# A two-block transformer on one core: the planner's clock gets a time for each change of the array's shape, products run in columns also behind scores, normed inputs use a form with two tensors

## The chip, the core and the metric

The kernel runs on one core of a Trainium2 chip. The core has TensorE (PE: matmuls, with its weight loads shown as PEld), VectorE (DVE), ScalarE (ACT), GpSimd (POOL) and SyncE (SP), which here issues the DMAs. The metric is the device time in microseconds of one execution; the median of three runs is given. Lower is better.

## What is computed

Two blocks, one after the other, over x of 32 samples x 128 tokens x 256 channels, in float32, with 16 heads of 16 channels. Each has self-attention, cross-attention to a context of 128 tokens, and a feed-forward layer with 1024 hidden channels:

```python
# block 0 (modulated by silu(cond) @ ada_w + ada_b)
xm1 = ln(x) * (1 + scale_sa) + shift_sa
x = x + gate_sa * (attn(qkv of xm1) @ sa_proj_w + sa_proj_b)
x = x + (attn(q of ln(x), k and v of context, mask) @ ca_proj_w + ca_proj_b)
x = x + gate_ff * (gelu(xm3 @ fc1_w + fc1_b) @ fc2_w + fc2_b)   # xm3: ln(x), modulated
# block 1 (gamma, beta from cond; rotated q and k)
x = x + attn(rope(q), rope(k), v of adaln1(x)) @ sa_out_w.T
x = x + attn(rope(q of adaln2(x)), rope(k), v of context) @ ca_out_w.T
x = x + (gelu(adaln3(x) @ ffn_w1.T + ffn_b1) @ ffn_w2.T + ffn_b2)
# ln(x) = (x - mean) / sqrt(var + eps); attn is a softmax over 128 keys
```

## The kernel before

The 32 samples are 16 groups of two (256 token columns each). A group goes through a block as a stream; eight streams are under way at once, on eight sets of buffers. Each stream is a Python generator that yields whenever it needs an engine. At building, a planner (`Tasks.run`, lines 150 to 176) keeps all waiting steps, asks a model clock (`Clock`, lines 42 to 102) when each could start, and emits the step that could start first; so the order of every engine's instructions is fixed before the kernel runs, and the chip only keeps its dependencies. For every 40 us of planned time a number of the table `ORDER` (line 35) seeds small changes of rank (`changed`) and, by `seed % 4`, a patience: how much later than the earliest a step may start and still be chosen by rank.

What the clock charges on TensorE depends on the shape in which the array is used:
- **full**: a 128x128 tile. `multiply` (line 258) writes the products of weights and activations this way at L264; transposes of normed inputs (L586) and of score maxima (L774) are also full.
- **rows**: 32x128 tiles. The scores (L749): four heads stand on 32 partitions each, 16 matmuls for one batch and pass.
- **columns**: 128x32 tiles. exp times values (L795), and products that follow them: at L262 `multiply` splits a product into four matmuls of 32 output partitions.

A step whose shape is "any" takes columns if the array is in columns, otherwise full:

```python
if way == "any":
    way = "columns" if self.way == "columns" else "full"
took = took * self.PACE + (self.TURN[self.way] if way != self.way else 0.0)
```

`rows_T`, `values` and `project` use it; a long row of products behind exp times values therefore stays in columns until something else comes.

Attention of one sample and one stage runs twice through one shared scores buffer of four PSUM banks: scores (L749), maxima by VectorE (L761), their transpose (L774), subtraction from the queries (L778), scores again in the other direction (L749), exp by ScalarE (L787), exp times values (L795), copy out by ScalarE (L801). The sums of the softmax go through DMAs (a strided copy, L818's reciprocal, a store and a broadcast load) before L829 multiplies them in. Four PSUM buffers (`mms`) are shared by all products and transposes.

Before each stage `normed_T` (from line 554) norms x: statistics on VectorE (L561, L562), the power -1/2 on GpSimd (L566, L568), then for each of two samples x minus mean times the reciprocal deviation on VectorE (L574), and `transposed` transposes the four 128x128 parts on TensorE (L586); L604, L606 or L596 write them to SBUF.

The trace shows a float32 product as two matmul records (eight in columns), and 32 records for a group of 16 score matmuls; a transpose has one.

Of the kernel before, what the change touches and what calls it, by code (L numbers as in the profile page):

```python
# [13 lines left out]
ALU = mybir.AluOpType  # L14
# [3 lines left out]
P = 128  # L18
B, S, D, H, HD, DF = 32, 128, 256, 16, 16, 1024
# [13 lines left out]

EVERY = 40.0
ORDER = (
    71372, 36752, 0, 0, 71454, 91697, 0, 94157, 73524, 26634, 81926, 67541, 0, 14443, 0, 59342, 0, 88828, 0,
    12337, 30536, 2421, 29624, 8901, 84470, 22357, 96881, 43920, 51881, 25816, 98785, 9044, 8412, 0, 96954, 9117,
    0
)


class Clock:

    HOP, DRAIN, TABLE, PACE = 0.06, 0.22, 1.28, 1.03
    TURN = {"full": 0.1, "rows": 0.15, "columns": 0.15}

    def __init__(self):
        self.free = dict.fromkeys(("pe", "dve", "act", "pool", "sp", "none"), 0.0)  # L50
        many = {"sc": 1, "mm": 4, "pt": 2, "set": NA, "qa": 2, "ou": 3, "st": 2, "ht": 1,
                "y": 3, "cx": 3, "x": NS + 1}
        self.slots = {kind: [0.0] * n for kind, n in many.items()}
        self.table, self.way = None, "full"
        self.now = 0.0
        self.moved = 0.0
        self.landed = 2.0

    def use(self, engine, took, way="full"):

        if engine in ("exp", "gelu"):
            if engine != self.table:
                took += self.TABLE
                self.table = engine
            engine = "act"
        if engine == "pe":
            if way == "any":
                way = "columns" if self.way == "columns" else "full"
            took = took * self.PACE + (self.TURN[self.way] if way != self.way else 0.0)
            self.way = way  # L70
        self.free[engine] = max(self.now, self.free[engine]) + took
        return self.free[engine] + (self.DRAIN if engine == "pe" else self.HOP)

    def dma(self, took):

        start = max(self.now, self.free["sp"])
        self.free["sp"] = start + 0.64
        self.moved = max(self.moved, start + 0.9) + max(0.1, took - 1.4)
        return self.moved + 0.5
# [40 lines left out]
def when(t):  # L120
    return t() if callable(t) else t
# [6 lines left out]
class Tasks:  # L128
# [21 lines left out]
    def run(self):  # L150
        clock = self.clock
        while self.waiting:

            first, chosen = {}, {}
            at = int(min(t for e, t in clock.free.items() if e in ("pe", "dve", "act")) / EVERY)
            seed = ORDER[at] if at < len(ORDER) else 0
            patience = (0.02, 0.02, 0.3, 0.8)[seed % 4]
            for task in self.waiting:
                ready, engine, kinds, rank = task[1]
                start, late = max(when(ready), clock.slot(kinds)), 0.0  # L160
                if engine in ("exp", "gelu"):
                    late = 0.0 if engine == clock.table else clock.TABLE
                    engine = "act"
                start = max(start, clock.free[engine])
                first.setdefault(engine, []).append((start, late, rank, task))
            for engine, l in first.items():
                horizon = min(start + late for start, late, _, _ in l)
                l = [(late, self.changed(task, rank, seed), task[2].turn(), start, i) for i, (start, late, rank, task) in enumerate(l)
                     if start + late <= horizon + patience]
                late, _, _, start, i = min(l)  # L170
                chosen[engine] = (start, first[engine][i][3])
            start, task = min(chosen.values(), key=lambda c: c[0])
            assert start < NEVER
            clock.now = start
            self.waiting.remove(task)
            self.step(task)
# [54 lines left out]
def two_blocks(ctx: ExitStack, tc: tile.TileContext, a: dict, out: bass.AP):  # L231
    nc = tc.nc
# [8 lines left out]
    clock = Clock()  # L241
# [15 lines left out]

    def multiply(to, lhs, rhs, start=True, stop=True):

        if clock.way == "columns":  # L260
            for j in range(0, P, 32):
                nc.tensor.matmul(to[j:j + 32], lhsT=lhs[:, j:j + 32], rhs=rhs, start=start, stop=stop)  # L262
        else:
            nc.tensor.matmul(to, lhsT=lhs, rhs=rhs, start=start, stop=stop)  # L264
# [51 lines left out]
    rows = const.tile([P, C + 2], F32, name="rows")  # L316
# [237 lines left out]
    def normed_T(wm, x, ready, eps, mod, g, name):  # L554


        mv = p_s.tile([P, GB, 2], F32, tag="mv", name=f"mv_{name}")
        yield ready, "dve", "", 1
        for b in range(GB):
            st = p_s.tile([P, 6], F32, tag="st", name=f"st_{name}_{b}")  # L560
            nc.vector.bn_stats(st, x[:, b, :])  # L561
            nc.vector.bn_aggr(mv[:, b, :], st)  # L562
        t = clock.use("dve", 1.17)
        yield t, "pool", "", 1
        ve = p_s.tile([P, GB], F32, tag="ve", name=f"ve_{name}")
        nc.gpsimd.tensor_scalar(ve, mv[:, :, 1], eps, None, ALU.add)  # L566
        rstd = p_s.tile([P, GB], F32, tag="rstd", name=f"rstd_{name}")
        nc.gpsimd.tensor_tensor(rstd, ve, neg_half, ALU.pow)  # L568
        t = clock.use("pool", 1.0)
        yield t, "dve", "y", 0  # L570
        y = clock.take("y")
        xn = ys[y]
        for b in range(GB):
            nc.vector.tensor_scalar(xn[:, b, :], x[:, b, :], mv[:, b, 0:1], rstd[:, b:b + 1],  # L574
                                    ALU.subtract, ALU.mult)
        t = clock.use("dve", 0.75)
        return (yield from transposed(wm, y, t, mod, g))

    def transposed(wm, y, t, mod, g):
        to, xn = wm.xt, ys[y]  # L580
        yield (lambda: when(t) if mod is None or mod in mods else NEVER), "pe", "mm", 1
        slot = clock.take("mm")
        ps = mms[slot].rearrange("p (c b s) -> p c b s", c=KC, s=S)
        for c in range(KC):
            for b in range(GB):
                nc.tensor.transpose(ps[:, c, b, :], xn[:, b, c * P:(c + 1) * P], ident)  # L586
        t = clock.use("pe", 0.45)
        clock.give("y", y, t)
        there = Event()

        def evict():

            engine = "act" if mod is None else clock.freer("act", "dve")
            yield t, engine, "", 1
            if mod is None:
                nc.scalar.copy(to.rearrange("p c (b s) -> p c b s", s=S), ps)  # L596
            else:
                scale, shift = mods[mod]
                for c in range(KC):
                    for b in range(GB):  # L600
                        at = g * GB + b
                        one, by, to_add = to[:, c, b * S:(b + 1) * S], scale[:, c, at:at + 1], shift[:, c, at:at + 1]
                        if engine == "act":
                            nc.scalar.activation(one, ps[:, c, b, :], AF.Identity, bias=to_add, scale=by)  # L604
                        else:
                            nc.vector.tensor_scalar(one, ps[:, c, b, :], by, to_add, ALU.mult, ALU.add)  # L606
            clock.give("mm", slot, there.add(clock.use(engine, 0.6 if mod is None else 1.45)))

        tasks.spawn(evict(), wm)
        return there  # L610
# [128 lines left out]
    def attention(wm, hd, masked, t, t_v, name, done):  # L739
# [3 lines left out]
        turned_top, second = [Event() for _ in range(GB)], [Event() for _ in range(GB)]  # L743
# [9 lines left out]
        def batch(b):  # L753
# [4 lines left out]
            end = group_rows(scs[slot], lambda p, c: q[p, c, cut], lambda p, c: k[p, c, cut])  # L758
# [13 lines left out]
                ou.append(clock.take("ou"))  # L772
            ps = mms[at][:, 0:S]
            nc.tensor.transpose(ps, top.rearrange("p r i -> p (r i)"), ident)  # L774
            end = turned_top[b].add(clock.use("pe", 0.12) + 0.1)
            yield end, "dve", "", 0
            qa = qas[less]
            nc.vector.tensor_tensor(qa, q[:, :, cut], ps.unsqueeze(1).to_broadcast([P, C, S]), ALU.subtract)  # L778
            end = clock.use("dve", 0.7)
# [3 lines left out]
            end = second[b].add(group_rows(scs[slot], lambda p, c: k[p, c, cut], lambda p, c: qa[p, c, :]))  # L783
# [4 lines left out]
            end = clock.use("exp", 1.98)  # L788
# [9 lines left out]
            end = last.add(clock.use("pe", 0.87, "columns") + 0.1)  # L798
# [3 lines left out]
            end = clock.use("act", 0.6)  # L802
# [30 lines left out]
        for b in range(GB):  # L833
            tasks.spawn(batch(b), wm)
# [301 lines left out]
```

## Time and profile before

| | us |
|---|---|
| median of 3 runs | 1459.13 (1456.2 to 1461.75) |
| the profiled execution | 1462.32 |
| its span, first to last instruction | 1460.5 |
| first matmul record, start of the last one | 1.3, 1455.9 |

The span is that of the instructions; the execution's time has a little around it. The page's chain of work that ended last lies 83% on TensorE. The costliest groups, by busy time in us, count and mean:

| group | busy | count | mean ns |
|---|---|---|---|
| DVE L761, maxima of scores | 300.6 | 256 | 1216 |
| ACT L787, exp | 248.3 | 256 | 1023 |
| PE L264, second feed-forward product | 193.4 | 848 | 382 |
| PE L749, scores, the two directions | 151.1 and 150.8 | 4096 each | 284 |
| PE L795, exp times values | 139.0 | 4096 | 278 |
| DVE L778, queries less maxima | 86.1 | 128 | 675 |
| POOL L729, rotated sums | 83.0 | 64 | 1299 |

A matmul's duration in this trace is modelled and overlaps with the next, so the distance from start to start is what counts on TensorE. Busy times of groups are unions: an operation that began while the one ahead was still running is not counted twice.

### The profile page before, as it was taken

Reading aid. Unit: us, or ns where it says so; the run is one execution under the profiler, and the core shown is the slowest. Engines: PE = TensorE matmul, PEld = TensorE weight load, DVE = VectorE, ACT = ScalarE, POOL = GpSimd, SP = SyncE. Lnnn points to the kernel's source line nnn. Section 1 sums busy time; section 2 is a strip of 40 time slices with the busy share of each in tenths; the row PEclk is TensorE's granted clock in tenths of the full one; section 3 lists DMA queues with packets and bytes.
Section 4 is the critical chain, followed back from the end, with each engine's and each line's share of the span. In section 5 each row is a group of like instructions: output and inputs, shape, how many; then the busy total and the mean of one; then the engine's idle time right before and its main releaser. Section 6 shows DMA issues by size and latency. Waiting matters only on the chain.

```text
span 1460.5 us, 45118 instructions
## 1 busy us (share of the span) xinstructions
PE 1425.4 (98%) x19764; PEld 1136.3 (78%) x19764; DVE 889.2 (61%) x1538; ACT 707.5 (48%) x1130; POOL 357.2 (24%) x498
## 2 busy tenths in 40 slices
PE   9999999999999999999999999999999999999998
PEld 7877778877777777667877777878788788777777
DVE  6656575665655665646565667667756557664641
ACT  6544464465465545445444544434454444535452
POOL 3122213332223314331223222122121212111111
PEclk9999999999999999999999999999999999999999
DMA  7253222233122242223313313032122212321110
GB/s 229 79 157 86 68 75 70 82 102 103 50 75 65 82 125 86 85 64 96 111 50 117 121 57 108 30 98 93 62 68 74 81 45 67 100 74 43 49 61 22
DMA packets 107380, 120.85 MB, mean 83 GB/s; under 512 B 11632, under 2 KB 82992, under 8 KB 107184
## 3 DMA queue, kind: packets, MB, share of 16 engines
q1 hardware_dynamic: 107184, 117.98, 26.1%
q8 instruction: 155, 2.54, 0.7%
q14 instruction: 41, 0.34, 0.1%
HBM read 54.92 MB, written 12.68 MB: 46 GB/s over the span
## 4 chain that ended last, share of the span: by engine, by line
PE 83%; DVE 6%; DMA 5%; ACT 2%; POOL 2%; issue 1%; SPq 1%; DVEq 0%; ACTq 0%; POOLq 0%
PE products L264 42%; PE scores L749 16%; PE products L262 11%; PE products L795 7%; PE products L586 3%; DVE top L761 2%; PE products L774 1%; DMA y<-gate_dram_sa 1%; ACT exp L787 1%; DVE y L574 1%; DMA ou<-inv_e 1%; DVE st L724 1%; DVE xt L829 1%; DMA ou<-inv_a 1%; PE products L475 1%
## 5 line engine op out<-in xcount | busy, mean ns | idle before, releaser
L761 DVE TENSOR_REDUCE top<-scores 128x8 f32<-128x1024 f32 x256 | 300.6, 1216 | 63.1 <-PE scores L749 60.2
L787 ACT ACTIVATE exp<-scores 128x1024 f32<-128x1024 f32 x256 | 248.3, 1023 | 168.3 <-PE scores L749 157.6
L264 PE MATMUL products<-w_ffn_w,ht 128*128 128x256 f32 x848 | 193.4, 382 | 0.0
L893 ACT ACTIVATE ht<-products,cols 128x256 f32<-128x256 f32 x256 | 117.2, 474 | 129.8 <-PE products L264 113.9
L264 PE MATMUL products<-xt,w_ffn_w 128*128 128x256 f32 x760 | 176.7, 383 | 0.4 <-DVE x L869 0.4
L264 PEld LDWEIGHTS products<-w_ffn_w,ht 128*128 128x128 f32 x848 | 158.5, 190 | 23.1
L749 PEld LDWEIGHTS scores<-qa,keys 32*128 32x128 f32 x4096 | 126.7, 187 | 48.1 <-issue 23.3
L749 PE MATMUL scores<-qa,keys 32*128 32x128 f32 x4096 | 151.1, 284 | 7.3 <-ACT exp L787 3.5
L264 PEld LDWEIGHTS products<-xt,w_ffn_w 128*128 128x128 f32 x760 | 140.8, 190 | 22.2 <-DVE x L869 0.8
L801 ACT COPY ou<-products 128x512 f32<-128x512 f32 x128 | 75.5, 591 | 166.7 <-PE products L795 157.9
L749 PEld LDWEIGHTS scores<-keys,queries 32*128 32x128 f32 x4096 | 126.4, 187 | 37.3 <-issue 19.5
L749 PE MATMUL scores<-keys,queries 32*128 32x128 f32 x4096 | 150.8, 284 | 3.3 <-ACT exp L787 3.2
L729 POOL TENSOR_TENSOR st<-st 128x512 f32<-128x512 f32 x64 | 83.0, 1299 | 234.1 <-DVE st L724 223.0
L795 PE MATMUL products<-exp,values 128*32 128x128 f32 x4096 | 139.0, 278 | 0.0
L778 DVE TENSOR_TENSOR qa<-queries,products 128x512 f32<-128x512 f32 x128 | 86.1, 675 | 66.3 <-PE products L774 65.7
L795 PEld LDWEIGHTS products<-exp,values 128*32 128x32 f32 x4096 | 106.7, 110 | 22.8 <-issue 11.1
L869 DVE TENSOR_TENSOR x<-products,x 128x512 f32<-128x512 f32 x64 | 43.9, 688 | 103.9 <-PE products L264 75.9
L829 DVE TENSOR_TENSOR xt<-xt,ou 128x512 f32<-128x512 f32 x64 | 49.3, 770 | 87.3 <-DMA ou<-inv_d 29.8
L724 DVE TENSOR_TENSOR st<-products,rope 128x512 f32<-128x512 f32 x128 | 81.4, 680 | 23.8 <-PE products L264 8.2
L264 PE MATMUL products<-xt,w_qkv_w 128*128 128x256 f32 x336 | 83.2, 394 | 0.8 <-DVE xt L606 0.8
L644 ACT COPY values<-products 128x512 f32<-128x512 f32 x64 | 40.4, 631 | 89.5 <-PE products L264 70.8
L877 POOL TENSOR_TENSOR x<-y,x 128x512 f32<-128x512 f32 x32 | 40.8, 1276 | 164.1 <-DVE y L873 164.0
(129 smaller groups left out, 1970.8 us busy)
## 6 DMA issues: line engine op xcount, KB each, us to landing
xt<-ou SPq DMA_DIRECT2D x64, 256.0 KB, 2.4
keys<-st SPq DMA_DIRECT2D x96, 128.0 KB, 2.1
queries<-st SPq DMA_DIRECT2D x96, 128.0 KB, 2.2
cxt<-in_ctx SPq DMA_DIRECT2D x32, 256.0 KB, 3.7
x<-in_x SPq DMA_DIRECT2D x16, 256.0 KB, 4.1
keys<-st SPq DMA_DIRECT2D x16, 256.0 KB, 2.7
y<-gate_dram_sa SPq DMA_DIRECT2D x16, 256.0 KB, 3.8
ou<-inv_a SPq DMA_DIRECT2D x32, 128.0 KB, 2.6
```

What stands on the lines that cost most here:

```text
L262: nc.tensor.matmul(to[j:j + 32], lhsT=lhs[:, j:j + 32], rhs=rhs, start=start, stop=stop)
L264: nc.tensor.matmul(to, lhsT=lhs, rhs=rhs, start=start, stop=stop)
L724: nc.vector.tensor_tensor(st[:, :, :, one], ps[:, :, one].unsqueeze(2).to_broadcast([P, 2, 2, S]), rope, ALU.mult)
L729: nc.gpsimd.tensor_tensor(st[:, 0], st[:, 0], st[:, 1], ALU.add)
L749: nc.tensor.matmul(sc[:, r, c * S:(c + 1) * S], lhsT=lhs(slice(32 * r, 32 * r + 32), c), rhs=rhs(slice(32 * r, 32 * r + 32), c), start=Tru ...
L761: nc.vector.tensor_reduce(top[:, r:r + 2, TOP:TOP + 2 * C:2], scs[slot][:, r:r + 2, :].rearrange("p r (c s) -> p r c s", s=S), AX.X, ALU.max)
L778: nc.vector.tensor_tensor(qa, q[:, :, cut], ps.unsqueeze(1).to_broadcast([P, C, S]), ALU.subtract)
L787: nc.scalar.activation(exps[pt][r // 2], scs[slot][:, r:r + 2, :], AF.Exp, scale=SCALE)
L795: nc.tensor.matmul(mms[at][32 * r:32 * r + 32, c * S:(c + 1) * S], lhsT=v[:, b, i:i + HD, :].rearrange("p d t -> p (d t)"), rhs=exps[pt][r ...
L801: nc.scalar.copy(ous[ou[0]][:, :, cut], mms[at].rearrange("p (c s) -> p c s", s=S))
L829: nc.vector.tensor_tensor(wm.xt, wm.xt, by, ALU.mult)
L893: nc.scalar.activation(ht[f // (FC // 2)][:, f % (FC // 2), :], ps[:, 0, :], AF.Gelu, bias=b1[:, f:f + 1])
```

## The change

Three things, in one diff. The clock's table of changes gets one time for each pair of shapes instead of one for each shape that is left, with two more shapes: "parts" (products in columns) and "turned" (transposes, which leave the array full); the general factor on TensorE's times goes from 1.03 to 1.015, and the table of seeds is another one. A product takes columns also if the array is in parts or, in stretches of 40 us whose seed asks for it (`lean`), if it stands in rows. And the normed inputs are computed by scalar_tensor_tensor: (x - mean) times the reciprocal deviation, the latter read as a tensor of 256 equal columns instead of as a scalar of each partition. Lines behind the edits move down: L264 is L275 in the changed kernel, L262 L273, L574 L586, L586 L598, L749 L761, L774 L786, L787 L799, L795 L807.

```diff
 ORDER = (
-    71372, 36752, 0, 0, 71454, 91697, 0, 94157, 73524, 26634, 81926, 67541, 0, 14443, 0, 59342, 0, 88828, 0,
...
+    38718, 32014, 0, 87893, 99950, 56838, 0, 53341, 21925, 7768, 6954, 0, 63578, 91846, 41557, 5424, 0, 45477, 0,
...
-    HOP, DRAIN, TABLE, PACE = 0.06, 0.22, 1.28, 1.03
-    TURN = {"full": 0.1, "rows": 0.15, "columns": 0.15}
+    HOP, DRAIN, TABLE, PACE = 0.06, 0.22, 1.28, 1.015
+    TURN = {
+        ("full", "rows"): 0.1, ("full", "columns"): 0.1, ("full", "parts"): 0.1,
+        ("rows", "full"): 0.26, ("rows", "turned"): 0.18, ("rows", "columns"): 0.15, ("rows", "parts"): 0.15,
+        ("columns", "full"): 0.26, ("columns", "turned"): 0.18, ("columns", "rows"): 0.15,
+        ("parts", "full"): 0.32, ("parts", "turned"): 0.24, ("parts", "rows"): 0.21,
+    }
...
-        self.table, self.way = None, "full"
+        self.table, self.way, self.lean = None, "full", False
...
             if way == "any":
-                way = "columns" if self.way == "columns" else "full"
-            took = took * self.PACE + (self.TURN[self.way] if way != self.way else 0.0)
-            self.way = way
+                way = "parts" if self.in_parts() else "full"
+            took = took * self.PACE + self.TURN.get((self.way, way), 0.0)
+            self.way = "full" if way == "turned" else way
...
+    def in_parts(self):
+
+        return self.way in ("columns", "parts") or self.way == "rows" and self.lean
...
             patience = (0.02, 0.02, 0.3, 0.8)[seed % 4]
+            clock.lean = seed // 4 % 4 == 3
...
-        if clock.way == "columns":
+        if clock.in_parts():
             for j in range(0, P, 32):
                 nc.tensor.matmul(to[j:j + 32], lhsT=lhs[:, j:j + 32], rhs=rhs, start=start, stop=stop)
...
-            nc.vector.tensor_scalar(xn[:, b, :], x[:, b, :], mv[:, b, 0:1], rstd[:, b:b + 1],
-                                    ALU.subtract, ALU.mult)
+
+            nc.vector.scalar_tensor_tensor(xn[:, b, :], x[:, b, :], mv[:, b, 0:1],
+                                           rstd[:, b:b + 1].to_broadcast([P, D]), ALU.subtract, ALU.mult)
...
-        t = clock.use("pe", 0.45)
+        t = clock.use("pe", 0.45, "turned")
...
-            end = turned_top[b].add(clock.use("pe", 0.12) + 0.1)
+            end = turned_top[b].add(clock.use("pe", 0.12, "turned") + 0.1)
```

More of the change, by code (lines that the diff above doesn't have):

```diff
@@ L35 @@
 ORDER = (
-    71372, 36752, 0, 0, 71454, 91697, 0, 94157, 73524, 26634, 81926, 67541, 0, 14443, 0, 59342, 0, 88828, 0,
-    12337, 30536, 2421, 29624, 8901, 84470, 22357, 96881, 43920, 51881, 25816, 98785, 9044, 8412, 0, 96954, 9117,
-    0
+    38718, 32014, 0, 87893, 99950, 56838, 0, 53341, 21925, 7768, 6954, 0, 63578, 91846, 41557, 5424, 0, 45477, 0,
+    75801, 0, 86349, 57432, 99928, 14485, 81598, 5044, 38730, 0, 40902, 37263, 32089, 83999, 84738, 0, 0, 0
 )
 class Clock:
-    HOP, DRAIN, TABLE, PACE = 0.06, 0.22, 1.28, 1.03
-    TURN = {"full": 0.1, "rows": 0.15, "columns": 0.15}
+    HOP, DRAIN, TABLE, PACE = 0.06, 0.22, 1.28, 1.015
[5 more added lines that the diff above has]
+    }
     def __init__(self):
```

## The prediction

> **What bounds the kernel now.** I read the page's busy times first, then TensorE's timeline in a stretch with every kind of work, then the windows with the granted clock, then who waited for the normed inputs.
>
> ```profile
> PE 1425.4 (98%) x19764; PEld 1136.3 (78%) x19764; DVE 889.2 (61%) x1538; ACT 707.5 (48%) x1130; POOL 357.2 (24%) x498
> ```
>
> TensorE is busy for 98% of the span, in every fortieth of it. VectorE is at 61%. So the time is TensorE's own work, plus what a change of the array's shape costs, plus the moments in which it waits. The timeline gives the price of all three. A product has two matmul records as one full matmul, eight as four column pieces; the columns below are start, duration, group, records.
>
> ```profile
> 734.46 3.62 PE L264 MATMUL products<-w_ffn_w,ht 128*128 128x256 f32 x16
> 738.01 1.17 PE L749 MATMUL scores<-qa,keys 32*128 32x128 f32 x32
> 739.11 3.72 PE L264 MATMUL products<-w_ffn_w,ht 128*128 128x256 f32 x16
> 742.76 1.17 PE L749 MATMUL scores<-keys,queries 32*128 32x128 f32 x32
> ...
> 748.05 1.08 PE L795 MATMUL products<-exp,values 128*32 128x128 f32 x32
> 748.95 1.91 PE L262 MATMUL products<-w_qkv_w,xt 128*32 128x256 f32 x32
> 750.79 1.17 PE L749 MATMUL scores<-qa,keys 32*128 32x128 f32 x32
> ...
> 755.42 1.08 PE L795 MATMUL products<-exp,values 128*32 128x128 f32 x32
> 756.43 0.66 PE L586 MATMUL products<-ident,y 128*128 128x128 f32 x4
> 756.92 0.38 PE L264 MATMUL products<-w_qkv_w,xt 128*128 128x256 f32 x1
> ```
>
> Subtract starts, not durations (ends are modelled). Within a group, starts of full records are 0.216 us apart in the trace; a column product takes the same 0.432 us. Then:
> - Scores: 738.01 to 739.11, 1.10 us, the same whatever follows (746.95 to 748.05 too).
> - Eight full products are 16 x 0.216 = 3.456. From 734.46 to 738.01 they take 3.55: leaving full for rows costs 0.094. From 739.11 to 742.76, entered from scores, 3.65: entering costs another 0.101.
> - exp times values, 32 x 0.027 = 0.864: 0.90 from 748.05 (entering columns from rows 0.033, going on in columns nothing), 1.01 from 755.42 (0.033, and 0.113 for leaving columns).
> - Four column products are 1.728: 1.84 from 748.95, so entering from columns is free and leaving costs 0.112.
> - Four transposes behind another shape: 756.43 to 756.92, 0.49 less 4 x 0.109 = 0.055.
>
> Summed over the order of before: products 2048 x 0.432 = 885; scores 256 x 1.103 = 282; exp times values 128 x 0.864 = 111; 512 transposes x 0.109 = 56; small ones 12; changes of shape beside those inside the scores 57. That is 1402.5 us without a wait. From the first matmul record (1.3 us) to the last one's start (1455.9) are 1454.6 us. So **52 us** are waits and slow clock: all that a better order could win beside the changes of shape.
>
> ```profile
> 10.00:17.00 7.00, 6.18 (x16) 4.73 (x15) 4.96 (x17) 6.40 (x9) 1.84 (x4) 0.51 0.84 287
> 105.00:113.00 8.00, 6.81 (x101) 5.66 (x102) 2.55 (x8) 4.14 (x6) 3.62 (x6) 0.57 0.33 100
> 1324.00:1328.00 4.00, 3.60 (x52) 2.58 (x55) 4.00 (x7) 0.61 (x2) 1.75 (x3) 0.57 0.00 0
> ```
>
> The windows show (seventh entry, granted clock) three stretches at half clock: about 6.8, 6.8 and 3.4 us long, so some 3.4 + 3.4 + 1.7 = 8.5 of the 52 us. About 43 us are plain waits.
>
> **The clock's table, and the order that comes of it.** The table costs nothing itself; it changes which task is issued next on every queue, SP's and POOL's too. Work is conserved: the built programs have the same 4096 score matmuls, 2048 of exp times values, 384 + 128 transposes and 2048 products, of which 458 were in columns and 524 will be; two table loads fewer on ScalarE, eight activations moved to VectorE (0.4 us each), nothing against their idle shares; SP issues the same 725 copies in another sequence, and no transfer grows. The changes of shape on TensorE, counted in the two built orders:
> - rows to full 189 becomes 153, rows to columns 67 becomes 103, columns to full 48 becomes 65, full to columns 46 becomes 30, full to rows 191 becomes 188, columns to rows 65 becomes 68. In all 606 becomes 607.
> - Leaving full 19 fewer x 0.094 = -1.8; leaving columns 20 more x 0.113 = +2.3; products entered from rows 20 fewer x 0.101 = -2.0; transposes entered from another shape 4 fewer, small ones 5 more, x 0.055 = +0.1; columns entered from rows or full 20 more x 0.033 = +0.7. Sum **-0.8 us**.
>
> **Products in columns behind scores.** 25 products follow scores in columns, which before never has. Unknown is their entry. Floor 0.033 (exp times values behind scores: same 128x32 tiles); ceiling 0.101 (a full product behind scores). I take 0.033, since what is loaded first is 32 columns wide; the ceiling adds 25 x 0.068 = 1.7 and makes the sum +0.9. Either way nothing that a measurement sees: what is saved on entering is paid on leaving columns.
>
> **The normed inputs' form.** L574 now is a tensor-scalar with two per-partition scalars, 192 of them.
>
> ```profile
> L574 DVE TENSOR_SCALAR y<-x,mv_f,rstd_f x32: 313/412/1373, 842.8 to 1432.0; 128x256 f32<-128x256 f32 x32
> ...
>   PE products L586: 6.7, 10
>   PEld products L586: 6.0, 14
> ```
>
> Undisturbed it takes 0.41 us; the slow ones reach 1.4. The timeline says why: a POOL operation runs.
>
> ```profile
> 600.83 1.70 DVE L574 TENSOR_SCALAR y<-x,mv_c,rstd_c 128x256 f32<-128x256 f32 x2 [0.18 <-POOL rstd_c L568]
> ...
> 600.78 1.27 POOL L729 TENSOR_TENSOR st<-st 128x512 f32<-128x512 f32 x1
> ...
> 908.25 1.50 DVE L829 TENSOR_TENSOR xt<-xt,ou 128x512 f32<-128x512 f32 x1 [0.41 <-issue]
> ...
> 907.92 1.28 POOL L729 TENSOR_TENSOR st<-st 128x512 f32<-128x512 f32 x1 [2.03 <-DVE st L724]
> ```
>
> (L829 is the nearest row to the new form: a VectorE operation with two tensors in SBUF.) The pair at 600.83 takes 1.70 instead of 0.82; it stands until POOL is done at 602.05. The groups of L574 are busy 95.9 us, 17.4 over 192 x 0.409. If the new form were free of that, VectorE would win the 17.4. But L829 at 908.25 also stands until POOL ends at 909.20, and runs on for 0.55 us: 1.50 instead of 0.69. The Trainium skill ("SBUF — State Buffer", Who interferes with whom) says the same against this edit: a VectorE instruction with two SBUF inputs contends with a GpSimd instruction that reads SBUF. So I keep the 17.4. The new form's own length: L829 needs 0.69 for 512 elements, of which 0.53 at one element in 1/0.96 ns, so 0.16 + 0.27 = 0.43 for 256. The scalar operand comes on top: a 128x128 tensor-scalar with two of them takes 0.403 (L606) where 0.16 + 0.13 would do, so about 0.06 for one. 0.49 against 0.41: +0.08 each, **+15 us on VectorE** (by a lock-free form, 15 - 17 = -2 us). VectorE has 570 us idle. On the path lie the transposes: 24 times TensorE waited for this line (the two rows above, 12.7 us). 24 x 2 x 0.08 = 3.8 us; half of it I let later waits absorb, as TensorE waits some 90 times in all: **+1.9**. Floor -2 (free of the lock: 24 x 0.18 us of lock less 0.16, nearly nothing, rounded up), ceiling +15 (96 pairs x 0.16, none covered).
>
> **The waits of the new order.** A wait appears where too little TensorE work stands between the group that feeds a chain and the group that needs it. I laid the prices above along both orders and compared each cover with the shortest such chain in the trace (scores, reduce, transposed maxima 2.85 us; scores, exp, next scores 2.29; a product, GELU, the same PSUM buffer again 1.73; output copy, sums by DMA, projection 11.1). Before: 59 covers too short, 26 us missing in sum. After: 68, with 33 us. With 0.8 us of margin, for a VectorE or ScalarE queue that holds one operation more, 172 both times. The place moves: before lacks 12.5 us in the first 200 us and after 7.7; between 400 and 800 us before lacks 5.3, after 17.0; from 1200 on 5.4 against 5.2. I take the mean of +7 (bare) and -1 (with margin): **+3.1**. The bounds are the rivals below.
>
> One rule bears on it. The skill ("TensorE: Matmul & The Clock Gate", Why this matters for your kernels) says to avoid idle gaps over about 3 us, lest the clock halve. The trace is harsher: before 105 us the longest gap was 1.85 us (1.56 of the 3.4 us from 102.2 busy), before 1324 only 1.42 (1.74 of 3.4 busy). By the rule at most one cover of the new order (short by 3.2 us, near 626) could halve the clock; by the row also those near 407 (2.3 short) and 1236 (1.5 and 1.0). I keep the present number of drops, cost 0.
>
> **Sum:** -0.8 + 1.9 + 3.1 = +4.2 us against the profiled span of 1460.5. Its execution took 1462.3, 3 us over the median of 1459.1, within the spread of the runs shown (1456.2 to 1461.8); added to the median this is **1463 us**, 0.3% up: no change that can be told.
>
> **Rivals.**
> - Faster, 1447: the early stretch runs through (5 us less), the half clock at 105 and 1324 does not come back (5.1), the end is tighter (2). For it: those two drops follow thin covers that the new order does not have there. Against: the middle is thinner.
> - Slower, 1479: the covers between 400 and 800 us decide. There 11.7 us more are missing; if the gaps near 407 and 1236 also halve the clock for 6.8 us each (3.4 lost each) and nothing is won early, +18.5 with the other terms' +1. It decides from about 7 us of new waits on. For it: the nine more short covers, with the deepest on keys brought by DMA. Against: equal sums at 0.8 us margin.
> - Slower, 1474: the two-tensor form is uncovered everywhere, +15. For it only that normed inputs head each stage; against: 24 of 96 waits.
> - It does not do what it says: entry in columns costs 0.101, 1465, inside the first case.
>
> **Chances.** Under 0.5% (7.3 us) a measurement here can't be told from no change. No change, by my sum: 0.41 (own range 1452 to 1466). Faster: 0.25. Slower: 0.34, of which the covers 0.25 and the form 0.09. The range that leaves out about 2 in 10 is 1445 to 1479.
>
> **What would show it.** Scores followed by columns, then the starts: 0.033 or 0.101 on entering. L586's new form: 0.49 us undisturbed, over 1 us beside POOL; a flat 0.49 would make the lock step wrong. Waits of 40 to 50 us with the sum of the steps at 1401.6; half clock in windows near 407 or 1236, or nowhere but at the start. I am wrong if the waits move by over 10 us, which the counts of covers alone can't exclude.

## The result, and the profile after

The changed kernel takes **1453.22 us** (12 runs, 1449.83 to 1457.01), the kernel before beside it 1460.51 us (12 runs): ratio **0.9954**, 95% interval 0.9940 to 0.9967. It is 7.3 us faster where I had forecast 4 us slower. The profiled execution has a span of 1449.5 us, one of the shorter ones, against 1460.5 before.

From the page of the changed kernel, the busy times:

```profile
PE 1422.2 (98%) x20160; PEld 1124.9 (78%) x20160; DVE 900.0 (62%) x1546; ACT 701.1 (48%) x1120; POOL 363.6 (25%) x498
```

TensorE still is the bound. VectorE is 11 us busier: the line of the normed inputs takes 106.5 us where it took 95.8. The timeline of TensorE in the changed kernel (start, duration, group, records) has the new thing, products in columns (L273) behind scores (L761):

```profile
181.01 1.08 PE L807 MATMUL products<-exp,values 128*32 128x128 f32 x32
182.02 1.17 PE L761 MATMUL scores<-qa,keys 32*128 32x128 f32 x32
183.12 3.66 PE L273 MATMUL products<-w_ffn_w,ht 128*32 128x256 f32 x64
186.71 1.17 PE L761 MATMUL scores<-keys,queries 32*128 32x128 f32 x32
```

Starts again: eight products are 64 x 0.054 = 3.456 us and take 186.71 - 183.12 = 3.59. That is 0.134 over, of which leaving is the known 0.112, so entering costs 0.022. Over all 25 places the median is the same 0.023: a little under the floor that I took. Every other step has its price of before (scores 1.103, full entered from scores 0.101, and so on). So the two profiled executions part as follows, each with its own steps summed as in the prediction (for before they come to 1403.9 us here, 1.4 more than there):

| us | before | after | change |
|---|---|---|---|
| products, scores, exp times values, transposes | 1285.8 | 1285.8 | 0 |
| changes of shape, those inside the scores too | 118.1 | 117.0 | -1.1 |
| half clock (half of its stretches) | 8.5 | 6.8 | -1.7 |
| other waits | 42.2 | 34.2 | -8.0 |
| before the first record, after the last one's start | 5.9 | 5.7 | -0.2 |

All that counts is in the waits. By place, with the half clock, the two columns are 19.7 and 13.3 us in the first 200 us, 3.7 and 4.2 to 400, 12.7 and 10.6 to 800, 4.5 and 2.0 to 1200, and 10.3 and 11.0 behind. The early stretch won 6.4 where the covers had said 4.8; the middle, which was to lose 11.7, won 2.1. The windows of the changed kernel show its half clock (seventh entry):

```profile
10.00:17.00 7.00, 6.18 (x20) 4.46 (x19) 4.49 (x15) 6.70 (x10) 2.24 (x4) 0.62 0.84 284
350.00:353.50 3.50, 3.50 (x38) 2.83 (x38) 2.74 (x4) 1.51 (x4) 0.00 (x0) 0.53 0.45 118
1247.00:1251.00 4.00, 2.85 (x7) 2.35 (x8) 0.69 (x1) 1.24 (x2) 0.00 (x0) 0.57 0.36 106
```

The drops at 105 and 1324 us are gone, as the rival "faster" had it, but two others have come: near 350, which I had not named, and, as feared, behind the thin covers that I had put near 1236 (the covers' times leave out the waits: 407 there is 427 here). In the 3.4 us ahead of each, TensorE was busy for only 1.53 and 1.56 us.

And the covers that I had counted as too short between 400 and 800 us? The deepest, near 626 and 3.2 us short, left no wait that counts: from 600 to 700 us TensorE is busy for 99.31 us, before for 96.91. The next, near 407, was a transfer of keys for a score group, 2.3 us short. The same kernel's timeline, VectorE, SP and TensorE:

```profile
420.82 1.91 PE L273 MATMUL products<-xt,w_qkv_w 128*32 128x256 f32 x32
...
423.91 0.67 DVE L688 TENSOR_TENSOR st<-products,cols 128x512 f32<-128x512 f32 x1
...
424.64 0.50 SPq L696 DMA_DIRECT2D keys<-st  x1
...
425.59 1.89 PE L275 MATMUL products<-xt,w_qkv_w 128*128 128x256 f32 x8
...
427.32 0.27 PE L786 MATMUL products<-ident,top 128*128 128x128 f32 x1
...
427.52 1.17 PE L761 MATMUL scores<-keys,queries 32*128 32x128 f32 x32
```

The chain starts with the product's end at 422.6 and feeds the scores at 427.52. The products in front began at 425.59 and, with 8 x 0.216, one transpose of 0.109 and the change of shape, end when the scores begin: no wait. The chain took at most 4.9 us. I had set it at 7.4, the shortest time from product to scores that I saw in its 16 cases before; none of those had been tight. The trace of before held the chain's own length all the same. One of its cases, and the landing times of L684 from its source view:

```profile
394.25 1.05 PE L262 MATMUL products<-xt,w_qkv_w 128*32 128x256 f32 x16
...
395.36 0.99 DVE L673 TENSOR_SCALAR queries<-products,rows,c_q_even 128x256 f32<-128x256 f32 x2
396.28 0.68 DVE L676 TENSOR_TENSOR st<-products,cols 128x512 f32<-128x512 f32 x1
...
396.98 0.50 SPq L684 DMA_DIRECT2D keys<-st  x1
...
DMA to landing us min/median/max: 2.3/2.7/3.0
```

The product ends at 394.25 + 16 x 0.054 = 395.11; the issue at 396.98 and 2.3 to 3.0 us to the landing make 4.2 to 4.9 us.

### The profile page after: what moved, and what is told of

It reads as the page before. It is cut to its first block, busy times and chain, and to the rows that moved or that the text cites. A ratio compares the mean times of both kernels' runs of the same rounds, so it can differ in the third digit from the quotient of the medians.

```text
span 1449.5 us, 45874 instructions
## 1 busy us (share of the span) xinstructions
PE 1422.2 (98%) x20160; PEld 1124.9 (78%) x20160; DVE 900.0 (62%) x1546; ACT 701.1 (48%) x1120; POOL 363.6 (25%) x498
## 4 chain that ended last, share of the span: by engine, by line
PE 82%; DVE 6%; DMA 5%; issue 2%; POOL 2%; ACT 1%; SPq 1%; DVEq 0%; ACTq 0%; POOLq 0%
PE products L275 42%; PE scores L761 16%; PE products L273 13%; PE products L807 7%; PE products L598 3%; DVE top L773 2%; PE products L786 1%; DVE y L586 1%; ACT exp L799 1%; DMA few_b<-ou 1%; DVE qa L790 1%; DMA ou<-inv_b 1%; POOL x L867 1%; POOL gb_a L866 1%; DVE st L736 0%
## 5 line engine op out<-in xcount | busy, mean ns | idle before, releaser
L799 ACT ACTIVATE exp<-scores 128x1024 f32<-128x1024 f32 x256 | 248.4, 1023 | 150.5 <-PE scores L761 144.2
L275 PE MATMUL products<-w_ffn_w,ht 128*128 128x256 f32 x896 | 202.4, 381 | 0.0
L275 PEld LDWEIGHTS products<-w_ffn_w,ht 128*128 128x128 f32 x896 | 167.6, 190 | 23.6
L275 PE MATMUL products<-xt,w_ffn_w 128*128 128x256 f32 x720 | 165.2, 382 | 0.5 <-ACT xt L616 0.5
L761 PEld LDWEIGHTS scores<-qa,keys 32*128 32x128 f32 x4096 | 125.9, 186 | 46.0 <-issue 19.8
L761 PEld LDWEIGHTS scores<-keys,queries 32*128 32x128 f32 x4096 | 126.6, 187 | 37.8 <-issue 21.9
L761 PE MATMUL scores<-qa,keys 32*128 32x128 f32 x4096 | 150.2, 283 | 4.4 <-ACT exp L799 1.6
L761 PE MATMUL scores<-keys,queries 32*128 32x128 f32 x4096 | 151.1, 284 | 2.6 <-ACT exp L799 1.3
L275 PEld LDWEIGHTS products<-xt,w_ffn_w 128*128 128x128 f32 x720 | 134.2, 191 | 20.9 <-ACT xt L616 1.3
L807 PE MATMUL products<-exp,values 128*32 128x128 f32 x4096 | 136.5, 275 | 0.2 <-ACT exp L799 0.2
L807 PEld LDWEIGHTS products<-exp,values 128*32 128x32 f32 x4096 | 105.7, 109 | 18.9 <-issue 6.0
L275 PE MATMUL products<-xt,w_qkv_w 128*128 128x256 f32 x408 | 99.4, 389 | 0.8 <-DVE xt L618 0.8
L841 DVE TENSOR_TENSOR xt<-xt,ou 128x512 f32<-128x512 f32 x64 | 46.2, 723 | 74.5 <-DMA ou<-inv_e 20.6
```

What stands on the lines that cost most here:

```text
L761: nc.tensor.matmul(sc[:, r, c * S:(c + 1) * S], lhsT=lhs(slice(32 * r, 32 * r + 32), c), rhs=rhs(slice(32 * r, 32 * r + 32), c), start=Tru ...
L799: nc.scalar.activation(exps[pt][r // 2], scs[slot][:, r:r + 2, :], AF.Exp, scale=SCALE)
L807: nc.tensor.matmul(mms[at][32 * r:32 * r + 32, c * S:(c + 1) * S], lhsT=v[:, b, i:i + HD, :].rearrange("p d t -> p (d t)"), rhs=exps[pt][r ...
L841: nc.vector.tensor_tensor(wm.xt, wm.xt, by, ALU.mult)
```

## Experiments

**Theory** after the result: the re-dealt order brings the gain by its waits; the two other edits are worth nothing or cost a little. **Rivals**: the new form frees VectorE and GpSimd of each other; or columns behind scores carry it.

### One edit alone, one edit undone

form_alone is the kernel before with this edit, form_undone the changed kernel with the reverse; the planner's charges and so the orders stay.

```diff
-            nc.vector.tensor_scalar(xn[:, b, :], x[:, b, :], mv[:, b, 0:1], rstd[:, b:b + 1],
-                                    ALU.subtract, ALU.mult)
+
+            nc.vector.scalar_tensor_tensor(xn[:, b, :], x[:, b, :], mv[:, b, 0:1],
+                                           rstd[:, b:b + 1].to_broadcast([P, D]), ALU.subtract, ALU.mult)
```

> The kernel before with only the normed inputs' form changed; the order of every engine's instructions stays that of before. Theory (the gain comes from the re-dealt order and its waits): +2 us against before, between 0 and +5; the form 0.48 us undisturbed instead of 0.41, VectorE 10 to 15 us busier. Rival (the gain comes from the form, which frees VectorE and GpSimd of each other): -5 to -7 us.

> The changed kernel with only the normed inputs' form put back; its order stays. Theory (order): within 3 us of the changed kernel, rather faster, ratio to before near 0.994 to 0.996. Rival (form): the gain is gone, ratio to before 1.000.

Measured: form_alone 1464.72 us, ratio 1.0030 (1.0021 to 1.0039), that is +4.4 us; form_undone 1452.9 us, 0.9941 (0.9926 to 0.9957), within the interval of the changed kernel. The rival is out: on the order of before the form costs, and on the new one it brings nothing that can be told. The source view of the changed kernel (minimum, median and maximum in ns, then who waited for it, us and times) says how:

```profile
L586 DVE SCALAR_TENSOR_TENSOR y<-x,mv_d,rstd_d x32: 473/478/1498, 525.1 to 1170.8; 128x256 f32<-128x256 f32 x32
...
  PEld products L598: 8.2, 18
  PE products L598: 5.4, 8
```

0.48 us undisturbed against 0.41, and still up to 1.5: it waits for POOL as the old form did. With a POOL operation alongside, the mean is 0.83 us (64 of 192), before 0.80 (65). In form_alone TensorE waited 31 times, 18.0 us in all, for this line; before, 24 times and 12.7 us.

full_behind_scores is the changed kernel in its own order, but the 172 products behind scores are issued as full matmuls:

```diff
...
+            self.behind = way == "parts" and (self.way == "rows" or self.way == "parts" and self.behind)
             self.way = "full" if way == "turned" else way
...
-        if clock.in_parts():
+        if clock.in_parts() and clock.way != "rows" and not clock.behind:
```

> The changed kernel in its own order, but the 172 products that stand in columns behind scores are issued as full matmuls; the planner still charges them as columns. From the steps of the changed kernel's trace (entering columns from rows 0.023 us, full 0.101, leaving full for rows 0.094, columns 0.112, transposes behind columns 0.055, over 25 runs: 11 followed by scores +0.7 us, 11 by transposes -1.0, three others 0): -0.4 us against the changed kernel. Theory (these columns are worth nothing by themselves): ratio to before 0.994 to 0.997, as the changed kernel. Rival (columns behind scores carry the gain): ratio 0.998 to 1.001.

Measured: 1449.21 us, ratio 0.9909 (0.9893 to 0.9926). Both expectations miss: the kernel is better without these columns, by some 4 us (by the two ratios, 0.9909 and 0.9954, 6.6). The steps can't say why, their sum is the same.

### Both edits out, and seeds of the other clock

after_again repeats the changed kernel. order_alone has the changed order, full matmuls behind scores and the old form. The other two swap the tables of seeds:

```diff
 ORDER = (
-    38718, 32014, 0, 87893, 99950, 56838, 0, 53341, 21925, 7768, 6954, 0, 63578, 91846, 41557, 5424, 0, 45477, 0,
...
+    71372, 36752, 0, 0, 71454, 91697, 0, 94157, 73524, 26634, 81926, 67541, 0, 14443, 0, 59342, 0, 88828, 0,
...
```

> The changed kernel itself, beside the next three on one chip, as their measure. Ratio to before 0.994 to 0.997 as shown.

> The changed kernel's order with both of its other edits taken out: full matmuls behind scores, and the old form of the normed inputs. Theory (the two edits each cost a little, the order brings the gain, and they add): full_behind_scores less 2 us, ratio to before 0.988 to 0.991, 3 to 9 us under the changed kernel. Rival (the 0.9909 of full_behind_scores was a chip's or a draw's doing): no more than 2 us under the changed kernel beside it, 0.993 to 0.996.

> The changed kernel with the table of seeds of before: same clock, another order. Theory A (an order is a draw; a table of seeds fits one clock only): no better than before, ratio 0.998 to 1.010. Theory B (the finer times of the clock make better orders whatever the seeds): ratio 0.992 to 0.997.

> The kernel before with the changed kernel's table of seeds: old clock, old form, another order. Theory A: a draw, ratio 0.998 to 1.010, on either side of the kernel with the new clock and the old seeds. Theory B: slower than the changed kernel by as much as before is, ratio about 1.000 or more.

| kernel | us | ratio to before | 95% interval |
|---|---|---|---|
| after_again | 1454.60 | 0.9958 | 0.9943 to 0.9973 |
| order_alone | 1446.63 | 0.9908 | 0.9887 to 0.9929 |
| new_clock_old_seeds | 1536.16 | 1.0517 | 1.0487 to 1.0547 |
| old_clock_new_seeds | 1550.77 | 1.0614 | 1.0582 to 1.0645 |

order_alone, 8 us under the changed kernel beside it, beats both kernels. So the order gave 13 us here and the two edits take about half of it back. The swapped tables are far outside both expectations: a table of seeds is worth 76 to 90 us, and only with its own clock. Part of that is the half clock, for 68 and 82 us of their profiled executions, against 17 before: at half the stretch, 26 and 32 us. Theory B (finer times alone make good orders) is out. Not tried: both clocks without any seeds. So whether the finer times led to a better choice, or another choice under the old times would have done as well, stays open.

### Why do columns behind scores cost?

I laid full_behind_scores and the repeated changed kernel group by group, and form_undone and order_alone likewise. In both pairs full matmuls win time in the same three places, near 436, 562 and 667 us: 1.3, 1.6 and 1.2 us in one pair, 0.6, 1.3 and 0.7 in the other. (Against the first profile of the changed kernel it is 1.1, 1.6 and 0.9; that execution makes it up elsewhere, and the two spans are equal, 1449.5.) The first and the third are projections that wait for the softmax sums. In the first it is their transfer: the store of the inverses (L833), and then, when it has landed, the broadcast load (L838). SP's timeline there, of the repeated changed kernel, and then of full_behind_scores (its lines are two further down):

```profile
430.41 0.34 SPq L833 DMA_DIRECT2D inv_a<-few_a  x1
433.50 1.19 SPq L838 DMA_DIRECT2D ou<-inv_a  x2
```

```profile
429.54 0.34 SPq L835 DMA_DIRECT2D inv_a<-few_a  x1
431.10 1.19 SPq L840 DMA_DIRECT2D ou<-inv_a  x2
```

The same store needs 3.09 us and 1.56. The DMA view of just this stretch names the difference. Repeated changed kernel, 430.3 to 433.6:

```profile
q1 hardware_dynamic: 144, 0.07, 7.3%
q8 instruction: 1, 0.02, 2.5%
```

One packet of the queue "instruction" lies in it, 16 KB long and 1.3 us in the trace (431.09). In full_behind_scores none does. The other two places are alike. Near 562 the packet starts at 558.73, behind the store of sums at 558.30; the reciprocal that needs them begins 3.85 us after that store, against 2.02 in full_behind_scores. Near 667 it starts at 661.11, behind the store of inverses at 660.71; the next issue comes after 3.51 us, against 2.02. In full_behind_scores no such packet lies in either. On the pages this queue's packets go with TensorE's records: 155 for 19764 before, 158 for 20160 after, 150 for 19128 in full_behind_scores, about 128 records to a packet. I read them as the loads of TensorE's instructions. A product in columns needs four times as many of them, so the places of all later loads move.

That is a theory with a test: move the loads by tiny matmuls at the start, when TensorE waits for inputs (36 of them as shown, 20 in after_shift_16).

```diff
-    for _ in range(12):
+    for _ in range(8):
         nc.tensor.matmul(mms[0][:, 0:P], lhsT=ident, rhs=ident, start=True, stop=True)
+    for _ in range(36):
+        nc.tensor.matmul(mms[0][0:32, 0:4], lhsT=ident[:, 0:32], rhs=ident[:, 0:4], start=True, stop=True)
```

> The changed kernel with 32 more, tiny, matmuls among the warm-up ones at the start (eight of twelve large ones stay, 36 tiny ones follow); nothing else moves, but the places at which TensorE's instructions are loaded (16 KB, 64 float32 matmuls at a time) move by half a load. Theory L (columns behind scores cost because their extra instructions put loads onto the small transfers of the softmax sums near 428 and 556 us): the loads leave these places, 2 to 5 us less than the changed kernel, ratio 0.991 to 0.994. Rival M (the columns cost by themselves): 0.995 to 0.997 as the changed kernel.

> The same with 16 more tiny matmuls, a quarter of a load. Theory L: between 0.991 and 0.996, not the same as the shift by 32. Rival M: as the changed kernel, 0.995 to 0.997.

> full_behind_scores with the same 32 tiny matmuls. Theory L: it may lose what it had won, ratio 0.991 to 0.997. Rival M: 0.990 to 0.992, as without them.

> The kernel before with the same 32 tiny matmuls. Theory L: it moves too, by up to 5 us either way, ratio 0.996 to 1.004, more than the interval. Rival M: 1.000 within the interval.

| kernel | us | ratio to before | 95% interval |
|---|---|---|---|
| after_shift_32 | 1451.35 | 0.9946 | 0.9930 to 0.9962 |
| after_shift_16 | 1452.66 | 0.9955 | 0.9939 to 0.9971 |
| full_shift_32 | 1457.56 | 0.9980 | 0.9967 to 0.9992 |
| before_shift_32 | 1457.72 | 0.9988 | 0.9976 to 1.0000 |

The ratios alone decide little: after_shift_32 lies between both expectations' ranges, full_shift_32 outside both on the slow side, and the interval of before_shift_32 just touches 1.000. The 32 tiny matmuls do more than move loads. They take time that I had not reckoned with: laid beside their originals, the first transposes come 3.7 to 4.2 us later in all three. And the half clock changes: ahead of the last matmul the profiles of after_shift_32, full_shift_32 and before_shift_32 have 3.4, 3.4 and 0 us of it, their originals 17.1, 13.7 and 17.1. Why is not shown. The three places are free of both, since the clock is full there in each profile. At them after_shift_32 wins 1.4, 1.6 and 1.0 us (near 435, 559 and 663), the three places of full_behind_scores, and more elsewhere, much of it where the half clock near 350 and 1250 is gone. full_shift_32 loses 8 us, more than the start explains: 0.6, 1.0 and 0.6 us at the same three places, the rest elsewhere, which I did not trace. (Two of its twelve runs took 1451.2 and 1452.0 us, the others 1455.6 to 1459.5; what differs in those two is not shown.) SP's timeline at the first place, of after_shift_32 and of full_shift_32:

```profile
429.42 0.34 SPq L835 DMA_DIRECT2D inv_a<-few_a  x1
430.99 1.19 SPq L840 DMA_DIRECT2D ou<-inv_a  x2
```

```profile
432.07 0.34 SPq L837 DMA_DIRECT2D inv_a<-few_a  x1
434.45 0.56 SPq L842 DMA_DIRECT2D ou<-inv_a  x1
```

1.57 us without a load in between, 2.38 with one (at 432.41). All eight profiles of the changed order agree at this place: five have a load behind the store and need 2.38 to 3.10 us, three have none and need 1.56 or 1.57. So at the three places, some 4 us in all, columns behind scores cost in this kernel by where they put the instruction loads, not by a price of their own. Rival M is out for full_shift_32 even with the start's 0.3% added (0.993 to 0.995, measured from 0.9967 up); for the shift by 16 the two theories had left the same values open, and its ratio tells nothing. Its profile fits: at the first place a load still follows the store, which takes 2.70 us, and hardly any time is won there (0.3 us).

## Why the prediction was right or wrong

- **What bounds the kernel**: right. The no-wait sum and its prices held to 0.01 us a step in the changed kernel; what was to be won lay in the 52 us of waits and half clock.
- **Changes of shape, -0.8**: right, -1.1 in the profile; entry in columns from rows 0.023 where 0.033 was taken.
- **Columns behind scores, "nothing that a measurement sees"**: the steps are worth nothing, as said. The 4 us that full matmuls win back lie at three places with moved instruction loads, which no part of my sum contained.
- **The form, +1.9**: right in kind and nearly in size. Length 0.48 where 0.49 was worked out; the lock stayed (0.83 us beside POOL), as the row of L829 and the rule of the Trainium skill ("SBUF — State Buffer", Who interferes with whom) on two SBUF inputs had it; the line takes 15.1 us more on the order of before and 15.6 on the new one, where +15 stood. The length of one element, 1/0.96 ns, stood there without a row; the trace has it in L524 and L829, 0.42 us for 256 elements and 0.69 for 512. On the order of before the form costs 4.4 us (3.1 to 5.7), near the 3.8 us of the 24 waits before I halved them. In the changed order it is not told from nothing.
- **The waits of the new order, +3.1**: this step failed, and with it the sign. In the profiles the other waits fell by 8.0 us. As built, the order alone was worth -13 us (0.9908), with the other two edits -7. Two things were wrong in the step. First, as the length of a chain I took the shortest case seen before, from its first group to the group that uses it; where no case was tight that is only an upper bound. Keys by DMA were put at 7.4 us and did in 4.9, and the landings in the trace of before would have said 4.2 to 4.9. With the shortest cases of both traces, by my own count over the two orders, the missing cover is 7.0 us before and 6.4 after, and of the 17 us that the middle was to lack some 2 are left. Second, such a sum can't be the waits: other waits were 42 and 34 us. By the same count most of them come from chains that run longer than their shortest; I take queues on VectorE and ScalarE and late transfers for the causes, but traced only the three places above. Which chains the new order shortened in the early stretch stays open. The even counts at 0.8 us margin were a sign of this, and I should have read them as "can't tell" with a wide range around 0, instead of leaning to +3.
- **Half clock, 0 net**: nearly (-1.7 in the profile). The rows were the better guide than the rule of the Trainium skill ("TensorE: Matmul & The Clock Gate", Why this matters for your kernels) on gaps over about 3 us: the clock halved near 350 behind a longest gap of 1.40 us, with TensorE busy for 1.53 of the last 3.4 us.
- **Rivals**: "faster" had the right places for the early stretch and the two drops, and gave it 0.25. "It does not do what it says" with entry at 0.101 is excluded by the timeline. The slower one is too: the middle got better.
- **A reading**: the profiled execution of before, 1462.3, was not within the runs shown but 0.6 us above the slowest. Nothing hangs on it.

What can't be settled: how much of the 7.3 us is the order's own. The loads' places alone moved one order by 8 us, start included. With the start's 4 us, against before_shift_32 the shifted changed kernel is 6.4 us faster, but full_shift_32 equal to it; unshifted the same two are 7.3 and 11.5 faster than before. The shift also took half clock away, so these are not pure pairs. My estimate, the mean of these four, is that the order is better by some 6 us, by as much less or more as the loads and the half clock fall.

## What to carry to other kernels

Price the steps of the bounding engine from start to start in the timeline; that part of a forecast holds. Do not price the waits of a re-planned order by the shortest time from group to group in the old trace: where a chain was never tight, add up its own steps, to the landing of its transfer. Even so, a forecast of the waits deserves a range of some 10 us in 1450 around no change. When two builds differ by under 1% and in their number of instructions, shift the instruction loads before believing in either, and look at the clock and the start too, which the shift changed here.

## What the runs showed that I had not expected

- TensorE's instructions come by DMA in packets of 16 KB, one for about 128 matmul records with their weight loads. (That they are TensorE's is read from the counts.) They are on average 1.1 us long, and a small transfer under way waits: in the eleven profiles other than those of the swapped tables, it took 1.60 us from the issue of the store of the softmax inverses to the next issue (median of 243 without a load in between) and 2.42 us with one (128 cases). A longer stretch catches a load more easily; but with only those loads that began within the first 1.2 us, which nearly every stretch outlasts, the median is 2.81 us (55 cases).
- 32 tiny matmuls at the start change the time of an unchanged order by 0.7%: 0.9909 against 0.9980. Of that the start is 0.3% and the loads at the three places are 0.15%; the rest is not traced.
- The half clock that follows a poor stretch lasts 3.4 or 6.8 us in different executions of one kernel (near 350 us: 3.4 in one profile of the changed kernel, 6.8 in the other), which alone spreads its times by some 1.7 us, half of the difference.
